# A graph network on one core: the two weightings of an attention step put together, and the second output's gate put behind the first one's

## The chip, the cores and the metric

The kernel runs on one core of a Trainium2 chip. The core has five engines with instruction queues of their own: TensorE (matrix products, "PE" in the profile; its weight loads are shown as "PEld"), VectorE ("DVE"), ScalarE ("ACT"), GpSimd ("POOL") and SyncE ("SP", which here issues DMAs). The metric is the time of one execution on the device in microseconds (us). The kernel before took 2346.37 us as the median of three runs (2345.69 to 2347.04).

## The reference

Per row, a layer normalisation and a rectification come first, then a batch normalisation, a graph convolution, four layers, a second graph convolution, and two residual sums. Cut to the two parts that the change touches, a layer is:

```
q = (xb @ Wq).reshape(BS, -1, H, DH)             # 16 graphs of 64 rows, 8 heads of 64
k = (cond @ Wk).reshape(BS, -1, H, DH)           # 16 x 256 rows of context
v = (cond @ Wv).reshape(BS, -1, H, DH)
w = softmax(einsum('bnhd,bmhd->bhnm', q, k) * DH ** -0.5)
o = einsum('bhnm,bmhd->bnhd', w, v)              # the weighting
h = h + (o @ Wo)
u = _ln(h) @ geglu_w[i] + geglu_b[i]             # 1024 x 512 times 512 x 4096
val, gate = jnp.split(u, 2, axis=-1)
f = val * gelu(gate)
h = h + f @ ffo_w[i] + ffo_b[i]
```

All data are 32-bit floats. The four layers run with weights of their own; the context `cond` is the same in all.

## The kernel before, in words

The four layers follow each other in one program. In each, the attention runs over eight steps, one for every 128 rows (two graphs) of the 1024. The projection of keys and values for step g + 1 is spread over step g, so that TensorE has work while the softmax of step g runs on VectorE and ScalarE.

Keys and values are exact to 32 bits, though the products are of 12-bit operands: each operand is split into a high and a low part and a third one (names `ah`, `al`, `as` for the left side, `bh`, `bl`, `bs` for the right), and a unit (`Twelve`) adds three groups of four products into one PSUM bank. `begin` issues the first two groups and asks ScalarE to scale the bank in place; `end` issues the third group, which must wait for that scaling, and copies the result out on ScalarE or VectorE. Units are staggered: the begin of the next stands between a unit's begin and its end.

`mix` weights the values. TensorE turns four blocks of the softmax (`tr_pr`); ScalarE and VectorE copy them to `pT`, turned block by turned block, ScalarE the even ones and VectorE the odd ones. Then `weigh(0)` and `weigh(1)` issue the small products of the first and the second half of the heads into one bank (`po`), 64 columns wide; the profile shows 32 products for each half. The last instruction copies the bank to `oT` on VectorE. Three hooks give `mix` other TensorE work to place in between. In steps 0 to 6 the first hook ends the last key unit, the second is empty, and the third begins the first value unit (`v[0]`) of step g + 1. In step 7 the second hook begins a product of the next stage, and the other two are empty.

The gated projection's first quarter is computed from plain 32-bit products (`Quad`), its other three quarters (r = 1 to 3, four chunks c each, 48 chunks in the four layers) by the class `Chunk`. A chunk makes a value and a gate block of two outputs with seven products instead of eight, by sums of operands. Six of the products (numbers 0, 5, 6, 4, 1, 3) are split into three groups as above: `scale` and `scale_onto` issue two groups and a scaling on ScalarE or VectorE, `end` the third group. The seventh is a plain 32-bit product (line 1175). `steps` is a generator; the loop over chunks runs the first five stretches of chunk n + 1 between the last three of chunk n. The gate of the second output (`g1`) needs product 4 and is made from VectorE's sum; the gate of the first output (`g0`) needs product 3. Both are one ScalarE instruction, at line 1139, of 128 x 512 elements. VectorE then multiplies each gate with its value block, at lines 1178 and 1181 (`fT`). Before it, ScalarE and VectorE split the operands of the chunks to come (`gha`, `gla`, `ghb`, `glb`), and GpSimd finishes that split and sums operands.

Order on TensorE in these parts is the order of the code, since nearly all of its instructions, and those of ScalarE and VectorE in the chunks, are marked to be kept in program order (`pin`). Waits between engines are put in by the framework, which leaves out a wait that an earlier wait of the same engine already covers. Instructions not marked so, such as the split of the first output operand (`left_parts`: `ah_f` on ScalarE, `al_f` and `as_f` on VectorE), are placed by the framework's scheduler.

Of the kernel before, what the change touches and what calls it, by code (L numbers as in the profile page):

```python
# [26 lines left out]
def gnn_kernel(  # L27
# [82 lines left out]
    def bank(name):  # L110
        return psum.tile([P, 512], F32, tag="bank", name=name)

    def t512(name, dtype=F32):
        return work.tile([P, 512], dtype, tag="t512", name=name)
# [83 lines left out]
    def transposed(t, name, each=lambda ins: ins):  # L198

        pt = bank(f"tr_{name}")  # L200
        for k in range(4):
            transposed.last = each(nc.tensor.transpose(pt[:, k * P:(k + 1) * P],
                                                       t[:, k * P:(k + 1) * P], ident))
        return pt
# [513 lines left out]
    with ExitStack() as behind:  # L718
        for begun_by in (scaled_last, shifted_last):
            behind.enter_context(tc.issue_after(begun_by.ins))  # L720
        for t in range(ET):
            if t % (ET // (NB * KC)) == 0:
                next(steps)
            count(t)
        for _ in steps:
            pass
        first_v = bank("begun_v0")
        plain(first_v, raw_x[0, 0], 0, raw_wv, range(2))
        with tc.issue_after(load_dve.ins):
            for j in counted:  # L730
                if j % 2:
                    degrees(j // 2, C[j // 2], t512(f"part_{j // 2}"))
        with tc.issue_after(degrees.last.ins):
            plain(first_v, raw_x[0, 0], 0, raw_wv, range(2, KC))
        nc.scalar.copy(begun["v0"][0][:, 0, :], first_v)
# [66 lines left out]
    def acc_tile(name):  # L802
        return accs.tile([P, 512], F32, tag="acc", name=name)
# [54 lines left out]
    def mix(l, g, probs, v, hooks, each=pin):  # L858

        oT = t512(f"oT_{l}_{g}")  # L860
        po = bank(f"po_{l}_{g}")

        def weigh(c2, pTs):
            for a in range(2):
                c = 2 * c2 + a
                for b in range(2):
                    for m in range(MB):
                        for j in range(2):
                            n0 = c * P + b * NPG
                            at = (a * MB + m) * P + b * NPG  # L870
                            each(nc.tensor.matmul(
                                po[j * DH:(j + 1) * DH, n0:n0 + NPG],
                                v[b][:, m, c * P + j * DH:c * P + (j + 1) * DH],
                                pTs[j][:, at:at + NPG],
                                start=(m == 0), stop=(m == MB - 1)))

        turned = []
        for c2 in range(2):
            pTs = []
            for j in range(2):  # L880
                u = 2 * c2 + j
                pt = transposed(probs[u], f"pr_{l}_{g}_{u}", each)
                pT = t512(f"pT_{l}_{g}_{u}")
                if j:
                    nc.vector.tensor_copy(pT, pt)
                else:
                    nc.scalar.copy(pT, pt)
                pTs.append(pT)
            turned.append(pTs)
            hooks[c2]()  # L890
        weigh(0, turned[0])
        hooks[2]()
        weigh(1, turned[1])
        mix.last = nc.vector.tensor_copy(oT, po)  # L894
        return oT

# [174 lines left out]
    class Chunk:  # L1071
# [69 lines left out]
        def steps(self, sum_next):  # L1141


            n, bias = self.n, gcols[:, self.cv:self.cv + 1]

            def add(to, x, y):
                pin(nc.vector.tensor_tensor(to, x, y, OP.add))  # L1147

            self.banks = {}
            self.scale(0)  # L1150
            yield
            self.scale(5)
            yield
            s1, u2, u3 = (acc_tile(f"g{x}_{n}") for x in ("s1", "u2", "u3"))
            pin(nc.scalar.copy(s1, self.end(0)))
            self.scale(6)
            yield
            add(u2, self.end(5), s1)
            yield
            sum_next()  # L1160
            self.scale(4)
            add(u3, self.end(6), u2)
            self.scale_onto(1, s1)
            g1 = acc_tile(f"g1_{n}")
            d = self.end(4)
            add(g1, d, u3)
            self.gate(g1, g1)
            self.scale_onto(3, u3)
            yield
            a = self.end(1)  # L1170
            yield
            g0 = acc_tile(f"g0_{n}")
            self.gate(g0, self.end(3))
            for k in range(2):
                pin(nc.tensor.matmul(d, self.last[:, k, :], self.rights[2][:, k, :], start=False,
                                     stop=k == 1, skip_group_check=True))
            f0, f1 = self.f.of(self.c)
            pin(nc.vector.scalar_tensor_tensor(f0, a, bias, g0, OP.add, OP.mult))
            add(d, d, u2)
            yield  # L1180
            pin(nc.vector.scalar_tensor_tensor(f1, d, bias, g1, OP.add, OP.mult))
            self.f.store(self.c)
# [263 lines left out]
    for l in range(L):  # L1446
# [118 lines left out]
        for g in range(NG - 1):  # L1565
# [19 lines left out]
            k[-2].end()  # L1585
            v = values(l, g + 1, wv)
            oTs.append(mix(l, g, probs, vs.pop(g), (k[-1].end, nothing, v[0].begin)))
            if g == NG - 2:
                ln3_norm(g - 2, g - 1, behind=mix.last)
# [49 lines left out]
        quads[0].first()  # L1639
        quads[1].first()  # L1640
        oT = mix(l, g, probs, vs.pop(g), (nothing, quads[2].first, nothing), lambda ins: ins)
        ln3_norm(g - 1)
        attn_out(l, g, oT, wo)
# [321 lines left out]
```

## Time and profile before

| What | Value |
|---|---|
| Median of three runs | 2346.37 us |
| Lowest and highest run | 2345.69 and 2347.04 us |
| The profiled execution | 2345.76 us |
| Its span, first to last instruction | 2343.9 us |
| TensorE busy | 2312.5 us, 12272 products |
| VectorE busy | 1624.6 us |
| ScalarE busy | 1081.7 us |
| GpSimd busy | 800.3 us |
| Granted TensorE clock | 1.00 |

The rows in the sections below have these columns. In a timeline: start in us from the span's start, duration in us, engine, line of the code and operation, what is written and read (buffer numbers left out), shape, count of merged instructions, and in brackets the engine's idle time ahead and what ended it. In a table of windows: the stretch of time, its length, then the busy time and number of instructions of TensorE, its weight loader, VectorE, ScalarE and GpSimd, the granted clock, and the share and rate of the DMA engines. In a row of waits: who waited for whom, us in total, how often, and the longest. Durations of matrix products include their modelled latency, so that neighbours overlap; times from start to start are the ones to add up.

### The profile page before, as it was taken

The page shows a single profiled execution, that of the slowest core. Times are in us where ns is not written, and L with a number is a line of the kernel's source. Part 1 is how long each engine was busy: PE and PEld are TensorE (multiplying, and loading weights), DVE is VectorE, ACT ScalarE, POOL GpSimd, SP SyncE. Part 2 cuts the span into 40 slices and gives each one's busy share as a digit, 9 for nine tenths or more (in the row PEclk, how much of TensorE's full clock was granted, in tenths as well). Part 3 has the DMA queues.
Part 4 walks back from the last instruction along what each step waited for, and adds up shares of the span by engine and source line. Part 5 has one row for each costly group of instructions (what it writes and reads, how often), then busy time and mean ns, then how long its engine had stood idle before and what let it go on. Part 6 is the DMA issues. An engine that isn't in the chain of part 4 may idle for free. (4 is left out here: it accounts for less than half of the span.)

```text
span 2343.9 us, 33537 instructions
## 1 busy us (share of the span) xinstructions
PE 2312.5 (99%) x12272; PEld 1716.5 (73%) x12272; DVE 1624.6 (69%) x3036; ACT 1081.7 (46%) x2099; POOL 800.3 (34%) x719
## 2 busy tenths in 40 slices
PE   8999999999999999999999999999999999999999
PEld 5668887577877887477886888567786888657787
DVE  9875456888974455788985544788886544688964
ACT  7444454455244445455344444555334444455410
POOL 1133222385032224177022333169022223158211
PEclk9999999999999999999999999999999999999999
DMA  6052120245412101144522101133531111033550
GB/s 202 12 165 73 67 74 8 70 126 174 151 62 68 42 19 37 54 119 137 180 73 68 66 21 37 34 106 117 180 126 68 43 44 37 7 115 116 180 190 37
DMA packets 161066, 205.40 MB, mean 88 GB/s; under 512 B 11304, under 2 KB 101744, under 8 KB 160896
## 3 DMA queue, kind: packets, MB, share of 16 engines
q1 hardware_dynamic: 158800, 197.77, 26.1%
q0 software_dynamic: 1376, 4.30, 0.5%
q8 instruction: 101, 1.65, 0.3%
q10 hardware_dynamic: 720, 1.11, 0.1%
q14 instruction: 69, 0.57, 0.1%
HBM read 152.80 MB, written 50.34 MB: 87 GB/s over the span
## 5 line engine op out<-in xcount | busy, mean ns | idle before, releaser
L321 POOL TENSOR_TENSOR as_c<-ah_c,al_c 128x512 fp32r<-128x512 f32 x128 | 196.9, 1568 | 409.3 <-PE fy L1258 234.4
L378 ACT ACTIVATE v<-v 128x512 f32<-128x512 f32 x127 | 74.1, 583 | 220.6 <-PE v L367 218.4
L1258 PE MATMUL fy<-bh_wff,ah_f 128*128 128x512 f32 x512 | 159.2, 392 | 0.0
L1258 PE MATMUL fx<-bs_wff,as_f 128*128 128x512 f32 x512 | 157.8, 389 | 0.5 <-DVE as_f L318 0.5
L1258 PE MATMUL fy<-bl_wff,al_f 128*128 128x512 f32 x512 | 157.8, 389 | 0.0
L315 ACT ACTIVATE ah_f<-fr 128x1024 fp32r<-128x1024 f32 x64 | 67.6, 1060 | 176.4 <-PE fy L1258 116.4
L1126 ACT ACTIVATE g<-g 128x512 f32<-128x512 f32 x192 | 111.9, 583 | 78.7 <-PE g L1112 78.7
L367 PE MATMUL v<-bh_wv,ah_c 128*128 128x512 f32 x508 | 145.9, 409 | 0.0
L367 PE MATMUL v<-bs_wv,as_c 128*128 128x512 f32 x508 | 143.4, 404 | 0.0
L848 ACT ACTIVATE pr<-sc,nmax 128x256 f32<-128x256 f32 x256 | 118.3, 475 | 53.6 <-DVE nmax L843 53.1
L1112 PE MATMUL g<-gr,gsa 128*128 128x512 f32 x384 | 137.1, 438 | 3.8 <-ACT g L1126 3.7
L378 ACT ACTIVATE k<-k 128x512 f32<-128x512 f32 x125 | 72.7, 585 | 144.5 <-PE k L367 144.5
L367 PE MATMUL v<-bl_wv,al_c 128*128 128x512 f32 x508 | 136.4, 390 | 0.0
L367 PE MATMUL k<-ah_c,bh_wk 128*128 128x512 f32 x500 | 134.6, 391 | 0.0
L367 PE MATMUL k<-al_c,bl_wk 128*128 128x512 f32 x500 | 134.0, 390 | 0.0
L367 PE MATMUL k<-as_c,bs_wk 128*128 128x512 f32 x500 | 132.1, 395 | 0.0
L1063 POOL TENSOR_TENSOR gsa<-gha,gla 128x512 fp32r<-128x512 f32 x88 | 112.1, 1295 | 55.6 <-DVE gla L1060 53.2
L1139 ACT ACTIVATE g<-g,gcols 128x512 f32<-128x512 f32 x96 | 67.2, 700 | 128.8 <-DVE g L1147 125.7
L1112 PE MATMUL g<-gr,gha 128*128 128x512 f32 x384 | 120.8, 396 | 0.0
L383 DVE COPY kT<-k 128x512 f32<-128x512 f32 x54 | 37.4, 692 | 118.9 <-PE k L367 118.9
L1112 PE MATMUL g<-gl,gla 128*128 128x512 f32 x384 | 118.6, 390 | 0.0
L920 POOL TENSOR_TENSOR os<-oT 128x256 f32<-128x256 f32 x12 | 8.8, 733 | 318.8 <-DVE oT L894 318.8
(353 smaller groups left out, 5749.4 us busy)
## 6 DMA issues: line engine op xcount, KB each, us to landing
f_dram<-fT SPq DMA_DIRECT2D x128, 256.0 KB, 2.7
fr<-f_dram SPq DMA_DIRECT2D x64, 512.0 KB, 4.4
ct<-cond_dram SPq DMA_DIRECT2D x48, 512.0 KB, 4.0
wff<-in_L_gnn_ffo_w_dram SPq DMA_DIRECT2D x32, 512.0 KB, 5.9
gxb<-in_L_gnn_geglu_w_dram SPq DMA_DIRECT2D x96, 128.0 KB, 2.6
gxa<-in_L_gnn_geglu_w_dram SPq DMA_DIRECT2D x96, 128.0 KB, 2.6
cond<-in_L_gnn_cond_dram SPq DMA_DIRECT2D x32, 256.0 KB, 3.4
cond_dram<-ct SPq DMA_DIRECT2D x16, 512.0 KB, 3.9
```

What stands on the lines that cost most here:

```text
L315: nc.scalar.mul(twelve_bits(h), x, INWARD * TINY)
L321: nc.gpsimd.tensor_tensor(twelve_bits(s)[:, k, :], h[:, k, :], l[:, k, :], OP.subtract)
L367: pin(nc.tensor.matmul(self.bank, twelve_bits(left[k // 2])[:, k % 2, self.c * P:(self.c + 1) * P], twelve_bits(right[k // 2])[:, k % 2, : ...
L378: nc.scalar.mul(self.bank, self.bank, 1.0 + TINY)
L383: nc.vector.tensor_copy(self.to(), self.bank)
L848: nc.scalar.activation(pr3[:, a, :], ps3[:, a, :], AF.Exp, bias=nmax[:, a:a + 1], accum_out=tot[:, a:a + 1])
L920: t.tensor_tensor(s1, a21, a22, OP.add)
L1063: pin(t.tensor_tensor(s_at, h_at, l_at, OP.subtract))
L1112: pin(nc.tensor.matmul(to, self.part(i, which)[:, k, :], self.rights[i][which].bitcast(F32R)[:, k, :], start=start and k == 0, stop=stop a ...
L1126: pin(nc.scalar.mul(to, to, 1.0 + TINY))
L1139: pin(nc.scalar.activation(to, of, AF.Gelu, bias=gcols[:, cg:cg + 1]))
L1258: pin(nc.tensor.matmul(to, twelve_bits(left[which][0])[:, k, b * P:(b + 1) * P], twelve_bits(right[which])[:, k, :], start=u == 0 and whic ...
```

## The change

Two edits:

```diff
@@ mix @@
             turned.append(pTs)
             hooks[c2]()
-        weigh(0, turned[0])
         hooks[2]()
-        weigh(1, turned[1])
+        for c2, pTs in enumerate(turned):
+            weigh(c2, pTs)
         mix.last = nc.vector.tensor_copy(oT, po)
@@ Chunk.steps @@
             g1 = acc_tile(f"g1_{n}")
             d = self.end(4)
             add(g1, d, u3)
-            self.gate(g1, g1)
             self.scale_onto(3, u3)
             yield
             a = self.end(1)
             yield
             g0 = acc_tile(f"g0_{n}")
             self.gate(g0, self.end(3))
+            self.gate(g1, g1)
```

The first edit puts the third hook, the begin of the next value unit, ahead of both weightings. On TensorE, in step 0 of layer 0, four groups of the value unit `v_1_0` appear behind the last turned block (the difference of the two orders, + is the changed kernel):

```order
 L202 MATMUL tr_pr_0_2_15737<-ident,pr_0_2_15653 128x128 x4
 L202 MATMUL tr_pr_0_3_15744<-ident,pr_0_3_15663 128x128 x4
+L367 MATMUL v_1_0_15751<-bh_wv_0_15057,ah_c_1_0_15501 128x512 x2
+L367 MATMUL v_1_0_15751<-bh_wv_1_15058,ah_c_1_1_15502 128x512 x2
+L367 MATMUL v_1_0_15751<-bl_wv_0_15059,al_c_1_0_15503 128x512 x2
+L367 MATMUL v_1_0_15751<-bl_wv_1_15060,al_c_1_1_15504 128x512 x2
 L871 MATMUL po_0_15717<-pT_0_0_15723,v_begun_456 64x64
 L871 MATMUL po_0_15717<-pT_0_1_15730,v_begun_456 64x64
```

They leave their old place between the two halves of the weighting, on the same engine, a few rows on:

```order
 L871 MATMUL po_0_15717<-pT_0_0_15723,v_begun_457 64x64
 L871 MATMUL po_0_15717<-pT_0_1_15730,v_begun_457 64x64
-L367 MATMUL v_1_0_15767<-bh_wv_0_15057,ah_c_1_0_15501 128x512 x2
-L367 MATMUL v_1_0_15767<-bh_wv_1_15058,ah_c_1_1_15502 128x512 x2
-L367 MATMUL v_1_0_15767<-bl_wv_0_15059,al_c_1_0_15503 128x512 x2
-L367 MATMUL v_1_0_15767<-bl_wv_1_15060,al_c_1_1_15504 128x512 x2
 L871 MATMUL po_0_15717<-pT_0_2_15742,v_begun_456 64x64
 L871 MATMUL po_0_15717<-pT_0_3_15749,v_begun_456 64x64
```

The two halves now stand in one run of products. The same move stands in each of steps 0 to 6 of each layer, 28 times; step 7 keeps its order.

The second edit moves one gate on ScalarE. Before, in layer 0, from the chunk (r, c) = (2, 0) to (2, 1), with the engines that each instruction waits for in brackets (a number in a name is layer-less: `g_0_2_0` is of chunk (2, 0); line 1126 is a scaling, 1139 a gate, 1155 the copy of product 0):

```order
L1139 ACTIVATE g_0_1_3_18760<-g_0_1_3_18704,gcols 128x512 [waits PE_49]
L1126 ACTIVATE g_0_2_0_18780<-g_0_2_0_18780 128x512 [waits PE_49]
L1139 ACTIVATE g_0_2_0_18795<-g_0_2_0_18795,gcols 128x512 [waits DVE_49,Activation_49]
L1126 ACTIVATE g_0_2_1_18806<-g_0_2_1_18806 128x512 [waits PE_49]
L1059 ACTIVATE ghb_2_1_18813<-gxb_2_1_18645 128x512 [waits DMAHW4_49,DMAHW3_49]
L1126 ACTIVATE g_0_2_1_18819<-g_0_2_1_18819 128x512 [waits PE_49]
L1059 ACTIVATE gha_2_2_18825<-gxa_2_2_18735 128x1024 [waits DMAHW3_49,Pool_49]
L1155 COPY gs_0_2_1_18840<-g_0_2_1_18806 128x512 [waits PE_49]
L1126 ACTIVATE g_0_2_1_18846<-g_0_2_1_18846 128x512 [waits PE_49]
L1139 ACTIVATE g_0_2_0_18852<-g_0_2_0_18800,gcols 128x512 [waits PE_49]
```

The same stretch of ScalarE in the changed kernel:

```order
L1139 ACTIVATE g_0_1_3_18699<-g_0_1_3_18699,gcols 128x512 [waits DVE_49]
L1126 ACTIVATE g_0_2_0_18780<-g_0_2_0_18780 128x512 [waits PE_49]
L1126 ACTIVATE g_0_2_1_18805<-g_0_2_1_18805 128x512 [waits PE_49,Activation_49]
L1059 ACTIVATE ghb_2_1_18812<-gxb_2_1_18644 128x512 [waits DMAHW4_49,DMAHW3_49]
L1126 ACTIVATE g_0_2_1_18818<-g_0_2_1_18818 128x512 [waits DVE_49,PE_49]
L1059 ACTIVATE gha_2_2_18824<-gxa_2_2_18734 128x1024 [waits DMAHW3_49,Pool_49]
L1155 COPY gs_0_2_1_18839<-g_0_2_1_18805 128x512 [waits DVE_49,PE_49]
L1126 ACTIVATE g_0_2_1_18845<-g_0_2_1_18845 128x512 [waits DVE_49,PE_49]
L1139 ACTIVATE g_0_2_0_18851<-g_0_2_0_18799,gcols 128x512 [waits DVE_49,PE_49]
L1139 ACTIVATE g_0_2_0_18795<-g_0_2_0_18795,gcols 128x512 [waits DVE_49]
```

The gate with the wait for VectorE alone has moved from ahead of the next chunk's first scaling to behind the first output's gate. The four instructions on the way have got a VectorE wait of their own, which the old gate's wait had covered.

One instruction of VectorE moves by the scheduler's choice, once in each layer: the split `al_f` of the first output operand, in the third chunk of the last quarter. Before:

```order
L1147 TENSOR_TENSOR gu_0_3_2_19305<-g_0_3_2_19309,gu_0_3_2_19304 128x512
L1130 TENSOR_SCALAR g_0_3_2_19339<-g_0_3_2_19339,gs_0_3_2_19303 128x512
L1147 TENSOR_TENSOR g_0_3_2_19345<-g_0_3_2_19330,gu_0_3_2_19305 128x512
L1130 TENSOR_SCALAR g_0_3_2_19350<-g_0_3_2_19350,gu_0_3_2_19305 128x512
L1235 TENSOR_SCALAR bl_wff_1_19133<-wff_1_18991,bh_wff_1_19132 128x512
L316 TENSOR_SCALAR al_f_0_0_19376<-ah_f_0_0_19375,fr_0_19273 128x1024
```

The same place on VectorE in the changed kernel:

```order
L1147 TENSOR_TENSOR gu_0_3_2_19304<-g_0_3_2_19308,gu_0_3_2_19303 128x512
L316 TENSOR_SCALAR al_f_0_0_19375<-ah_f_0_0_19374,fr_0_19272 128x1024
L1130 TENSOR_SCALAR g_0_3_2_19339<-g_0_3_2_19339,gs_0_3_2_19302 128x512
L1147 TENSOR_TENSOR g_0_3_2_19345<-g_0_3_2_19330,gu_0_3_2_19304 128x512
L1130 TENSOR_SCALAR g_0_3_2_19349<-g_0_3_2_19349,gu_0_3_2_19304 128x512
L1235 TENSOR_SCALAR bl_wff_1_19132<-wff_1_18990,bh_wff_1_19131 128x512
```

It now stands ahead of the two scalings at line 1130 instead of behind them. GpSimd's and SyncE's orders are unchanged, and no instruction is added to the computation or taken from it; some of the added waits are carried by wait instructions of their own.

## The prediction

> **What bounds the kernel now.** I read the page first, then the waits of TensorE and of its weight loader, then the stretches of time in which the two edited places lie.
>
> ```profile
> span 2343.9 us, 33537 instructions
> ...
> PE 2312.5 (99%) x12272; PEld 1716.5 (73%) x12272; DVE 1624.6 (69%) x3036; ACT 1081.7 (46%) x2099; POOL 800.3 (34%) x719
> ```
>
> TensorE is busy for 99% of the span and no other engine for more than 69%, so only what shortens or lengthens TensorE's own chain counts. Two rows show what of that chain is not arithmetic: a wait, and the idle time of the weight loader ahead of the 64-column products of the attention (tile po).
>
> ```profile
> PE g L1112 <- ACT g L1126: 3.7, 4, 1.1
> ```
> ```profile
> PEld po L871 <- issue: 17.7, 60, 0.8
> ```
>
> The numbers are microseconds in total, times, and the longest. The first row is four waits, one per layer, in the gated projection, on a ScalarE instruction of the line that does the scalings. The second row has 60 entries: two in each of the 28 attention steps that the diff reorders, one in each of the 4 last steps, which it leaves alone. "issue" means that nothing was waited for: it is the price of a border between two kinds of product. So both edits touch places where TensorE loses time now.
>
> **The change, part one: the weightings of an attention step.** This is TensorE's order in one step of layer 1; the other steps repeat it.
>
> ```profile
> 749.34 1.03 PE L202 MATMUL tr_pr<-ident,pr 128*128 128x128 f32 x8
> 750.12 1.18 PE L367 MATMUL k<-as_c,bs_wk 128*128 128x512 f32 x4
> 751.14 1.03 PE L202 MATMUL tr_pr<-ident,pr 128*128 128x128 f32 x8
> 752.10 1.15 PE L871 MATMUL po<-pT,v 128*64 128x64 f32 x32
> 753.18 1.20 PE L367 MATMUL v<-bh_wv,ah_c 128*128 128x512 f32 x4
> 754.22 1.08 PE L367 MATMUL v<-bl_wv,al_c 128*128 128x512 f32 x4
> 755.23 1.15 PE L871 MATMUL po<-pT,v 128*64 128x64 f32 x32
> 756.31 1.19 PE L367 MATMUL v<-bh_wv,ah_c 128*128 128x512 f32 x4
> ```
>
> Ends are modelled, so I count from start to start. From the last eight transposes to the first product of the next value unit it takes 756.31 - 751.14 = 5.17 us: transposes 0.96, weighting 1.08, value unit 2.05, weighting 1.08. The edit puts the value unit ahead of the first weighting. The three pieces of the new order are all in the trace: eight transposes followed by a 512-column product take 750.12 - 749.34 = 0.78; the value unit, followed by a weighting, takes 755.23 - 753.18 = 2.05; and 64 weightings in one run stand in the last step of each layer:
>
> ```profile
> 2023.89 2.08 PE L871 MATMUL po<-pT,v 128*64 128x64 f32 x64
> 2025.90 1.12 PE L298 MATMUL ga<-ln3T,wval 128*128 128x512 f32 x2
> ```
>
> That is 2.01, against 2 x 1.08 in two runs. The sum is 0.78 + 2.05 + 2.01 = 4.84, a gain of 0.33 per step and of 28 x 0.33 = 9.2 us. Nothing is computed less; two of the four changes into and out of the narrow products are gone.
>
> The rule that speaks against it is in the Trainium skill, "TensorE: Matmul & The Clock Gate", Part 2, "Step-by-step: what each phase is for": the engine's queue pulls weight loads ahead of running matmuls, so that the next weights load behind the present product. By that alone a border would cost nothing and this part would be worth 0. The 17.7 us of the weight loader's row say otherwise, and "TensorEngine Tiling (Array Packing)", "Key Properties", says why: "Mode switching requires drain". By this rule the 9.2 us stand, and the trace sides with it.
>
> What could take the gain away is the data. The second half of the weighting needs the fourth turned block, which VectorE copies last:
>
> ```profile
> 753.15 0.69 DVE L885 COPY pT<-tr_pr 128x512 f32<-128x512 f32 x1
> ```
>
> It is there at 753.84. In the new order the second half starts at 751.14 + 0.78 + 2.05 + half of 2.01 = 754.97, so 1.13 us remain (1.39 today). The first half needs blocks copied earlier still. The value unit's own ScalarE scaling, due before that unit's third group, gets its input sooner than now. The orders of VectorE, ScalarE, POOL and SP in the attention do not move. One more wait, for a VectorE copy long done, goes ahead of the first weighting. The trace has no such wait at this border. Its bounds are 0 and 0.17 us a step, the latter the width of a whole border here (0.96 against 0.78 behind the transposes); I take 0, because TensorE drains there anyway. So the part is worth 4.5 to 9.8 us (the upper end if the value unit also starts 0.02 quicker, the 1.02 of the products at 750.12 against the 1.04 at 753.18).
>
> **Part two: the gate of the second output.** In the projection ScalarE now stands at the gate (line 1139) until VectorE has made its input, and the scaling of the next chunk's first product is queued behind it. Where VectorE is late, TensorE gets to the product's last group and finds it unscaled. First ScalarE, then TensorE, in the second chunk of layer 0:
>
> ```profile
> 470.36 0.72 ACT L1139 ACTIVATE g<-g,gcols 128x512 f32<-128x512 f32 x1 [3.92 <-DVE g L1147]
> 470.99 0.58 ACT L1126 ACTIVATE g<-g 128x512 f32<-128x512 f32 x1
> 471.50 0.61 ACT L1059 ACTIVATE ghb<-gxb 128x512 fp32r<-128x512 f32 x1
> ```
> ```profile
> 468.85 0.61 PE L1112 MATMUL g<-gl,gla 128*128 128x512 f32 x2
> ...
> 470.21 0.61 PE L1112 MATMUL g<-gr,gsb 128*128 128x512 f32 x2
> 471.71 0.70 PE L1112 MATMUL g<-gr,gsa 128*128 128x512 f32 x2 [0.88 <-ACT g L1126]
> ```
>
> The product to be scaled is done at 469.46; its scaling starts at 470.99, because the gate sat ahead of it. With the gate moved, the scaling can run at about 469.5 to 470.1, and the group at 471.71, due 0.45 after 470.21 (the spacing of the three groups from 468.85 on), meets no wait. The size is read from whole periods of a chunk (from one last product to the next), not from the wait alone, since the pipeline must refill too:
>
> ```profile
> 462.56:473.61 11.05, 10.17 (x41) 7.44 (x40) 8.18 (x11) 6.46 (x11) 9.03 (x11) 1.00 0.35 96
> 473.61:483.54 9.93, 9.93 (x42) 7.51 (x40) 8.52 (x11) 5.42 (x10) 7.91 (x9) 1.00 0.53 160
> ...
> 493.49:503.69 10.20, 10.17 (x42) 7.43 (x41) 9.51 (x12) 6.25 (x11) 8.25 (x9) 1.00 0.35 103
> ...
> 1004.32:1015.38 11.06, 10.19 (x41) 7.44 (x40) 8.18 (x11) 6.48 (x11) 9.03 (x11) 1.00 0.36 98
> 1546.09:1557.40 11.31, 10.17 (x41) 7.44 (x40) 7.88 (x11) 6.45 (x11) 9.28 (x11) 1.00 0.35 98
> 2087.84:2098.88 11.04, 10.18 (x41) 7.43 (x40) 8.21 (x11) 6.47 (x11) 9.01 (x11) 1.00 0.33 96
> ```
> ```profile
> 2118.75:2128.95 10.20, 10.19 (x42) 7.43 (x41) 9.52 (x12) 6.25 (x11) 8.25 (x9) 1.00 0.34 103
> ```
>
> An undisturbed period is 9.93. The first period of the four layers is longer by 1.12 + 1.13 + 1.38 + 1.11 = 4.74, and the fourth (first and last of four shown) by 0.27 in these two and by 0.82 in all four, by the same late gate. The sum is 5.5 us. The ends are 3.7 (the waits alone) and 6.0 (a few hundredths more in other chunks).
>
> What does the gate meet at its new place? It follows the first output's gate, and the scaling of the next sum stands behind it. The tightest case is a chunk in which ScalarE also splits an output weight; ScalarE, then VectorE's multiplication that needs the moved gate:
>
> ```profile
> 495.23 0.67 ACT L1139 ACTIVATE g<-g,gcols 128x512 f32<-128x512 f32 x1
> 496.78 0.58 ACT L1126 ACTIVATE g<-g 128x512 f32<-128x512 f32 x1 [0.88 <-PE g L1112]
> ```
> ```profile
> 497.80 0.74 DVE L1181 SCALAR_TENSOR_TENSOR fT<-g,gcols,g 128x512 f32<-128x512 f32 x1
> ```
>
> ScalarE idles 0.88 there for TensorE, and the gate takes 0.67 to 0.72: it ends near 496.6, 0.2 before the scaling can start and 1.2 before VectorE asks. Cost 0. In a layer's last chunk the moved gate delays the split of a later output operand by as much, behind which VectorE still has its own multiplications to do: 0 too.
>
> Two side effects. ScalarE's instructions that leaned on the old gate's wait now carry a VectorE wait of their own, about four per chunk, all for work of the chunk before. The nearest row is the split at 471.50, which waits for two DMAs: it starts 0.51 behind the start of a 0.58 us scaling, so at once. I price them at 0; the trace bounds it by ScalarE's idle time. And once per layer VectorE now does a 1.22 us split of the first output operand (al_f) ahead of, not behind, the scaling that an ending product (561.07) needs:
>
> ```profile
> 558.08 0.70 DVE L1130 SCALAR_TENSOR_TENSOR g<-g,gs 128x512 f32<-128x512 f32 x1
> ...
> 560.66 1.22 DVE L316 SCALAR_TENSOR_TENSOR al_f<-ah_f,fr 128x1024 fp32r<-128x1024 f32 x1
> ```
> ```profile
> 561.07 0.61 PE L1112 MATMUL g<-gr,gsb 128*128 128x512 f32 x2
> ```
>
> The scaling would end at 558.78 + 1.22 = 560.0 against 561.07: covered by 1.07. If that cover were gone, the four splits would cost at most 4.9 us.
>
> **The sum.** 9.2 + 5.5 = 14.7. The profiled execution took 2345.76 us (its span and 1.86 around it), so 2331.1; the median of the runs, 2346.37, stands 0.6 above it: 2331.7 us.
>
> **The rivals.** The gate's wait goes but VectorE's lateness shows at the next thing: TensorE then waits for a VectorE scaling instead. For it: VectorE is busy for 9.5 of 10.2 us in the slow fourth period. Against it: in the second chunk no wait for VectorE stands beside the ScalarE one. Then 2346.4 - 9.2 = 2337.2. Chance 8%.
>
> The added waits cost at the borders: attention 4.5, projection 4: 2337.9. Chance 6%. That such waits become instructions of their own is said by the Trainium skill, "Perfetto Trace Analysis", "Identifying Dependency Chains", without a price.
>
> Borders cost nothing in themselves, or the narrow products pay the same in one run: the attention keeps its time, 2340.9. Against it stands the 2.01. Chance 5%.
>
> Slower: the fourth turned block is late. VectorE copies it behind a 1.2 us split of the context; if the new timing held it up, each step would wait. The gain of a step is eaten at 1.13 + 0.33 = 1.46 us of delay, and at 1.13 + 0.33 + (5.5 + 4.7) / 28 = 1.82 us the kernel is 0.2% slower, 2351 or more. Nothing in the trace delays it so. Chance 4%.
>
> Neither edit moves TensorE's chain: 2346. Chance 4%.
>
> **How the numbers follow.** My case has 73%, its own range 2329.5 to 2334.5. Within 0.2% (4.7 us, about what a measurement tells from nothing) is 4%, slower 4%, and all the rest, 92%, is faster. The range 2329.5 to 2338.5 takes in my case and the two rivals near 2337 and leaves out the others.
>
> **What would show it.** The 32-product runs of po become runs of 64, the weight loader's idle row falls from 60 entries to 32 and to some 13 us; the row of TensorE's wait on the scaling disappears; the first chunk period falls from 11.05 to 9.93; TensorE's share stays at 99%. I am wrong if a wait of TensorE on VectorE's copies of the turned blocks appears, if the period between attention steps stays, or if the first chunk period keeps its length under another name.

## The result: 2330.35 us, 0.7% faster, and the profile after

The changed kernel takes 2330.35 us (median of 6 runs, 2329.82 to 2330.77) against 2346.27 us before (6 runs, 2345.65 to 2347.04). The ratio is 0.9931, 95% interval 0.9921 to 0.9942. The forecast was 2331.7, with a range of 2329.5 to 2338.5. The profiled execution took 2330.63 us, its span 2328.8. In the fences of this part are the rows of the changed kernel that answer to those shown of the kernel before. First its page:

```profile
span 2328.8 us, 33792 instructions
...
PE 2300.4 (99%) x12272; PEld 1714.9 (74%) x12272; DVE 1613.3 (69%) x3036; ACT 1078.3 (46%) x2099; POOL 817.7 (35%) x719
```

TensorE is still busy for 99% and still sets the time. It does the same 12272 products in 12.1 us less busy time; the 255 instructions more are waits that became instructions. Next the weight loader's idle time ahead of the narrow products (total, times, longest), and the waits of TensorE:

```profile
PEld po L871 <- issue: 13.2, 32, 0.8
```
```profile
PE gc L298 <- DVE gu L1013: 7.3, 4, 1.8
...
PE g L1112 <- DVE g L1130: 1.3, 4, 0.3
```

The loader's entries went from 60 to 32 and its 17.7 us to 13.2. In TensorE's list the row "g L1112 <- ACT g L1126" is gone (it held 3.7 us), no other row has taken its place, and no wait for a turned block is there. This is TensorE's order in one attention step, and then the stretches of the first and fourth chunk of layer 0 and the first of layer 1 (start and end, length, busy time of TensorE, weight loader, VectorE, ScalarE and GpSimd, granted clock, DMA share, GB/s):

```profile
747.62 1.03 PE L202 MATMUL tr_pr<-ident,pr 128*128 128x128 f32 x8
748.42 1.17 PE L367 MATMUL v<-bh_wv,ah_c 128*128 128x512 f32 x4
749.43 1.08 PE L367 MATMUL v<-bl_wv,al_c 128*128 128x512 f32 x4
750.44 2.08 PE L871 MATMUL po<-pT,v 128*64 128x64 f32 x64
752.45 1.20 PE L367 MATMUL v<-bh_wv,ah_c 128*128 128x512 f32 x4
```
```profile
460.97:470.90 9.93, 9.93 (x42) 7.51 (x40) 7.89 (x11) 6.64 (x11) 8.53 (x10) 1.00 0.28 83
...
490.75:500.68 9.93, 9.93 (x42) 7.51 (x40) 8.82 (x11) 6.28 (x11) 9.29 (x8) 1.00 0.35 105
...
998.73:1008.66 9.93, 9.93 (x42) 7.51 (x40) 7.89 (x11) 6.64 (x11) 8.53 (x10) 1.00 0.28 85
```

From the last eight transposes to the next value unit it takes 752.45 - 747.62 = 4.83 us; it was 5.17, and 4.84 was forecast. Every full chunk period is 9.93, where it was up to 11.31. Counted over the trace, the steps of the attention gave 9.7 us (from the transposes of a layer's first step to those of its eighth 2.43 less, four times) and the projection 6.0 (from the first chunk's last product to the twelfth's, a layer took 108.13 and takes 106.62). These are 15.7 of the 15.9 by which the medians differ; the spans differ by 15.0, since the profiled execution after had spent 0.85 more ahead of the first chunk (0.4 in a wait for VectorE at the start of the kernel, 0.5 in one ahead of tile gd in layer 0). In another profiled execution of the same kernel, below, that stretch was 0.8 shorter.

### The profile page after: what moved, and what is told of

Read it like the earlier page. It is cut to its first block, busy times and chain, and to the rows that moved or that the text cites. A ratio compares the mean times of both kernels' runs of the same rounds, so it can differ in the third digit from the quotient of the medians.

```text
span 2328.8 us, 33792 instructions
## 1 busy us (share of the span) xinstructions
PE 2300.4 (99%) x12272; PEld 1714.9 (74%) x12272; DVE 1613.3 (69%) x3036; ACT 1078.3 (46%) x2099; POOL 817.7 (35%) x719
## 5 line engine op out<-in xcount | busy, mean ns | idle before, releaser
L1126 ACT ACTIVATE g<-g 128x512 f32<-128x512 f32 x192 | 112.9, 588 | 191.9 <-PE g L1112 191.9
L1112 PE MATMUL g<-gr,gsa 128*128 128x512 f32 x384 | 136.2, 436 | 0.0
L1112 PE MATMUL g<-gr,gha 128*128 128x512 f32 x384 | 120.7, 395 | 0.0
L1112 PE MATMUL g<-gl,gla 128*128 128x512 f32 x384 | 118.6, 390 | 0.0
L1258 PEld LDWEIGHTS fy<-bh_wff,ah_f 128*128 128x128 f32 x512 | 96.1, 188 | 21.6 <-issue 1.9
```

The source lines that it names most:

```text
L1112: pin(nc.tensor.matmul(to, self.part(i, which)[:, k, :], self.rights[i][which].bitcast(F32R)[:, k, :], start=start and k == 0, stop=stop a ...
L1126: pin(nc.scalar.mul(to, to, 1.0 + TINY))
L1258: pin(nc.tensor.matmul(to, twelve_bits(left[which][0])[:, k, b * P:(b + 1) * P], twelve_bits(right[which])[:, k, :], start=u == 0 and whic ...
```

## The experiments

**Each edit alone.** The first run has only the edit of the attention, the second only that of the projection.

```diff
 # e1_mix: the kernel before, with
-        weigh(0, turned[0])
         hooks[2]()
-        weigh(1, turned[1])
+        for c2, pTs in enumerate(turned):
+            weigh(c2, pTs)
 # e2_gate: the kernel before, with
-            self.gate(g1, g1)
             self.scale_onto(3, u3)
...
             self.gate(g0, self.end(3))
+            self.gate(g1, g1)
```

> The kernel before with the first edit alone: the value unit ahead of both weightings, the gate left where it was. Theory (a removed pair of borders is worth 0.35 us in each of 28 steps, and has nothing to do with the projection): 9.9 us faster than before, 2346.3 - 9.9 = 2336.4, with the four waits of TensorE on the scaling (3.7 us) and first chunk periods of 11.0 to 11.3 still there. Rival (part of the 9.9 is only to be had together with the moved gate, for instance because the projection begins in another phase): less than 8 us, above 2338.

> The kernel before with the second edit alone: the gate moved, the two weightings on either side of the value unit as before. Theory (the gate held the scalings behind it, and every chunk that ran long ran long for that): 6.0 us faster, 2340.3, all chunk periods 9.93, no wait of TensorE on a scaling. Rival (only the waits that the profile lists are won, the rest came with the attention): 3.7 us, 2342.6.

Measured: 2336.75 us (ratio 0.9962, 0.9949 to 0.9976) and 2340.52 us (0.9976, 0.9967 to 0.9985) against 2346.43 before, so 9.7 and 5.9 us. Together that is 15.6, and both edits at once gave 15.9: they add up, and neither needs the other. In the first run's list of waits the row of the scaling stands, and its first chunk is as long as before:

```profile
PE g L1112 <- ACT g L1126: 3.4, 4, 0.9
```
```profile
460.74:471.79 11.05, 10.19 (x41) 7.44 (x40) 8.19 (x11) 6.47 (x11) 9.03 (x11) 1.00 0.33 96
```

In the second run it is gone with the attention as it was, so the projection's whole gain comes from the gate's place:

```profile
464.66:474.59 9.93, 9.93 (x42) 7.51 (x40) 7.89 (x11) 6.64 (x11) 8.53 (x10) 1.00 0.26 79
```

**More borders.** If a border has a price, putting more of them in has to cost it again. Here the 64 narrow products of a step are cut into four runs of 16.

```diff
 # e3_quarters: the changed kernel, with
         def weigh(c2, pTs):
             for a in range(2):
+                if len(hooks) > 3:
+                    hooks[3](2 * c2 + a)
...
-(k[-1].end, nothing, v[0].begin)
+(k[-1].end, nothing, nothing, v[0].quarter)
```

`quarter` issues two of the eight products of the value unit's begin, ahead of each run; its own code is not shown.

> The changed kernel with more borders: the 64 narrow products of each of the 28 steps in four runs of 16, with two of the value unit's eight products ahead of each run. The same products, the same data, later needed than made. Theory (a pair of borders has a price of its own, 0.35 us): three pairs more in each step, 28 x 3 x 0.35 = 29 us slower than the changed kernel, 2359.8, and slower than the kernel before; the weight loader's idle row of the narrow products is back with some 200 entries. Rival (the gain came from the place of the value unit or from what VectorE and ScalarE get done meanwhile, the borders being free): 2330.4 within 3 us.

Measured: 2359.93 us, ratio 1.0055 (1.0038 to 1.0072), 29.6 us more than the changed kernel. Over 28 x 3 = 84 pairs that is 0.35 a pair. TensorE's order, one step:

```profile
727.14 0.71 PE L386 MATMUL v<-bh_wv,ah_c 128*128 128x512 f32 x2
727.78 0.69 PE L888 MATMUL po<-pT,v 128*64 128x64 f32 x16
728.39 0.73 PE L386 MATMUL v<-bh_wv,ah_c 128*128 128x512 f32 x2
...
732.22 1.20 PE L367 MATMUL v<-bh_wv,ah_c 128*128 128x512 f32 x4
```
```profile
PEld po L888 <- issue: 33.6, 88, 0.8
...
PEld po L888 <- ACT pT L904: 10.2, 28, 0.4
```

TensorE's own list has no wait at any of these starts, and the step's piece takes 732.22 - 727.14 = 5.08 where the changed kernel takes 752.45 - 748.42 = 4.03. So the price belongs to the border itself, not to the place of the value unit. The loader's entries stand in two rows, 116 in all and not 200: four for each of the 28 steps and one for each of the 4 last. The second row names ScalarE's copy of a turned block for the first run of each step, but in this step that copy ended at 727.57, 0.2 ahead of the run's first load at 727.77, and the loader was idle for 0.36 there as at the three other runs. So this is no wait for data either. Together the rows hold 43.8 us, 30.6 more than in the changed kernel: here, with 512-column products on both sides of every run, the loader's idle time follows the price of 29.6 us.

**Only narrow products?** Transposes and 512-column products also differ in kind, but both use all 128 columns. Here sixteen transposes stand in one run.

```diff
 # e6_turns: the changed kernel, with
-(k[-1].end, nothing, v[0].begin)
+(nothing, k[-1].end, v[0].begin)
```

> The changed kernel with one more regrouping of the same kind: the four products that end the last key unit come behind the second eight transposes, not between the two groups of eight, so that a step has sixteen transposes in one run. Theory (each change of kind costs TensorE time, the narrow products being only the dearest): the four products between transposes take 1.01 us in a step against 0.91 between their like, so at least 0.10 a step is won, 28 x 0.10 = 2.8 us, 2327.6, and with a second border of the size of that one 5.6, 2324.8. Rival 1 (only the 64-column products pay at their borders): 2330.4, no change. Rival 2 (the second transposes now wait for their banks or the turned blocks come late): a wait of TensorE or longer steps, slower than 2331.

Measured: 2329.80 us, ratio 0.9929 (0.9915 to 0.9943), 0.5 below the changed kernel, within what these runs can tell apart. The trace gives 0.03 us a step:

```profile
717.10 1.91 PE L202 MATMUL tr_pr<-ident,pr 128*128 128x128 f32 x16
718.76 1.17 PE L367 MATMUL k<-as_c,bs_wk 128*128 128x512 f32 x4
...
721.68 2.08 PE L871 MATMUL po<-pT,v 128*64 128x64 f32 x64
```

The piece takes 721.68 - 717.10 = 4.58; in the changed kernel the same products take 4.61 (0.79 + 1.01 + 0.79 + 2.02). My 0.10 was misread: the 1.01 behind the transposes holds the tail of the eighth transpose, since eight of them take 0.79 ahead of another product and sixteen take 718.76 - 717.10 = 1.66, not 1.58. The first rival holds: of the borders tried, only those into and out of the 64-column products have a price. The Trainium skill, "TensorEngine Tiling (Array Packing)", "Key Properties", has it so: a change of the tiling mode drains TensorE. The trace agrees, with 0.35 for a pair of borders between the whole array (128*128 in the rows: transposes and 512-column products) and half its columns (128*64: the weightings), and 0.03 for a pair that stays on the whole array.

The weightings differ from their neighbours in two more ways, and the profile of the changed kernel has rows for both. They are plain 32-bit products between split ones. So are the four of line 1175 in a chunk, on the whole array:

```profile
500.68 1.88 PE L1175 MATMUL g<-ln3T,gy 128*128 128x512 f32 x4
501.99 1.02 PE L1112 MATMUL g<-gr,gsa 128*128 128x512 f32 x2
502.85 0.63 PE L1112 MATMUL g<-gr,gha 128*128 128x512 f32 x2
```

These six take 502.85 - 500.68 = 2.17. Four plain products among their like take 1.72 (427.18 to 428.90 in the same profile) and two split ones 0.46 (502.85 to 503.31), so nothing is left for this pair of borders. The weightings are also short. At 36.89, seven 16-bit products on the whole array, of 384, 352, 32, 288, 96, 224 and 160 columns, take 0.66 us up to the next product, and their starts lie 0.16, 0.15, 0.03, 0.12, 0.04 and 0.10 apart: the one of 32 columns between two long ones brings no pause, so a change of length alone has no such price there. What is left is the 64 columns of the array. No run changed these alone.

**How late may the fourth turned block be?** VectorE's copy is made twice, then four times.

```diff
 # e4_late1 (2) and e5_late3 (4): the changed kernel, with
                 if j:
-                    nc.vector.tensor_copy(pT, pt)
+                    for _ in range(2 if c2 and g < 7 else 1):
+                        nc.vector.tensor_copy(pT, pt)
```

> The changed kernel with VectorE's copies of the second output of each pair's later block made twice, so that the fourth turned block of each of the 28 steps is 0.65 us later. In the changed kernel it is there 0.1 to 0.2 us ahead of the first narrow product, the half that needs it starts 1.0 behind that: a margin of 1.1 to 1.2 us (0.65 in the first step of layer 0). Theory: the delay is covered, 2330.4 within 0.7 us. Rival (the margin is not where the start times put it, for instance since the narrow products of both halves are queued with one wait at the head): 28 x 0.5 = 14 us slower, about 2344.

> The same with that copy made four times: the fourth turned block is 1.95 us later in each of the 28 steps. Theory: 1.95 - 1.15 = 0.8 us are not covered, 28 x 0.8 = 22 us slower than the changed kernel, 2353, with a wait of TensorE on VectorE's copy in the trace. Rival 1 (the slack is wider): under 10 us slower. Rival 2 (no slack at all): 28 x 1.8 = 50 us slower, 2381.

Measured: 2330.41 us for the first (ratio 0.9929, 0.9913 to 0.9946): one copy more, 0.72 us, is covered as predicted. VectorE, then TensorE:

```profile
749.11 1.41 DVE L886 COPY pT<-tr_pr 128x512 f32<-128x512 f32 x2
```
```profile
749.91 2.08 PE L871 MATMUL po<-pT,v 128*64 128x64 f32 x64
751.93 1.20 PE L367 MATMUL v<-bh_wv,ah_c 128*128 128x512 f32 x4
```

The block is there at 750.52, 0.6 behind the start of the narrow products, and they take 2.02 all the same. Only the first step of layer 0, whose copy is later, lost 0.19.

The second took 2376.94 us (1.0129, 1.0112 to 1.0146), 46.6 more than the changed kernel and twice my 22. The wait has the name I gave it:

```profile
PE po L871 <- DVE pT L886: 32.4, 24, 2.4
```

The size has three parts. A copy takes 0.72 from start to start, not 0.65, so three take 2.16, and 1.1 was not covered in 12 of the steps. In 12 others VectorE's order itself changed in my kernel: one half of the context's split now stands between the copies, so the block was 1.2 later still and the step lost 2.2 (2.7 in layer 0's first). The 4 last steps lost 0.24. These make 26.6 + 13.4 + 1.0 = 41 us, as does the sum over all runs of narrow products in the trace. VectorE and TensorE in layer 1:

```profile
731.62 1.41 DVE L886 COPY pT<-tr_pr 128x512 f32<-128x512 f32 x2
732.95 1.26 DVE L316 SCALAR_TENSOR_TENSOR al_c<-ah_c,ct 128x1024 fp32r<-128x1024 f32 x1
734.13 1.40 DVE L886 COPY pT<-tr_pr 128x512 f32<-128x512 f32 x2
```
```profile
735.59 1.15 PE L871 MATMUL po<-pT,v 128*64 128x64 f32 x30 [1.90 <-DVE pT L886]
736.66 1.87 PE L367 MATMUL v<-bh_wv,ah_c 128*128 128x512 f32 x4
738.34 1.91 PE L367 MATMUL v<-bl_wv,al_c 128*128 128x512 f32 x4
```

The third part, some 4.7 us, is in the last two rows and is told at the end: TensorE's clock fell.

**The gate half way.** Which of the work behind the gate mattered?

```diff
 # e7_gate_mid: the changed kernel, with
             yield
+            self.gate(g1, g1)
             a = self.end(1)
...
             self.gate(g0, self.end(3))
-            self.gate(g1, g1)
```

> The changed kernel with the gate of the second output half way: in ScalarE's order behind the two scalings and the two splits that it stood ahead of before, but still ahead of the copy, the next scaling and the first output's gate. Theory (only the scalings queued right behind the gate mattered): as fast as the changed kernel, 2330.4, within 0.7 us; all chunk periods 9.93. Rival (the gate has to be out of the way of all that ScalarE does before the first output's gate, since VectorE is late by more than two scalings): it waits again in the first chunk of each layer, between 1 and 4.5 us slower, 2331.4 to 2334.9.

Measured: 2331.28 us (0.9941, 0.9927 to 0.9954), 0.9 above the changed kernel and a little outside the 0.7 that I allowed; its profiled execution has a span of 2328.4, no longer than 2328.8. First chunk, then ScalarE ahead of it:

```profile
460.18:470.18 10.00, 10.00 (x42) 7.52 (x41) 8.37 (x11) 6.64 (x11) 8.60 (x10) 1.00 0.25 75
```
```profile
460.36 1.06 ACT L1059 ACTIVATE gha<-gxa 128x1024 fp32r<-128x1024 f32 x1 [1.56 <-POOL gxa L1096]
461.33 0.71 ACT L1139 ACTIVATE g<-g,gcols 128x512 f32<-128x512 f32 x1
```

The gate starts right behind the split, without a wait of its own, and the first period of a layer is 10.00: four layers lose about 0.4 us, of 6.0. So the theory holds for nearly all of it: what the old gate cost was the two scalings and the two splits that stood right behind it. The other half microsecond of the median is not to be seen in the trace.

**A further version.** The score products (tile sc, 64 x 64) are narrow too. Two kernels put those of the next step right behind the weightings: in all steps, then only in three steps of a layer, with the sixteen transposes as above. The changed kernel ran again beside the second.

```diff
 # e8_joined: the changed kernel, with
-            probs = scores(l, g, qT, kTs.pop(g))
+            probs = scored or scores(l, g, qT, kTs.pop(g))
...
             oTs.append(mix(l, g, probs, vs.pop(g), (k[-1].end, nothing, v[0].begin)))
+            scored = scores(l, g + 1, qT, kTs.pop(g + 1))
 # e9_joined_even: the same for g in (0, 2, 4), and
-(k[-1].end, nothing, v[0].begin)
+(nothing, k[-1].end, v[0].begin)
```

> The changed kernel with the 32 score products of the next step (tile sc, 64 rows by 64 columns) put right behind the 64 weighting products, instead of behind the value units, so that the narrow products of a step stand in one stretch. Theory (a border between 128-column and 64-column products has a price, 0.35 a pair for po, some 0.25 for sc, 1.00 + 1.05 against 2 x 0.91 for the products around them): one pair of the two goes and a smaller border between the two narrow kinds stays, 0.1 to 0.3 us a step won, 3 to 8 us, 2322 to 2328, if ScalarE's eight exponentials, which now stand ahead of the scalings of the value units, are done in time. Rival (they are not, and TensorE waits for the scaling of a value unit or for a bank): slower than 2332.

> The changed kernel with two regroupings: the next step's score products right behind the weightings in the three steps of a layer (0, 2, 4) that have no output products behind them, and the sixteen transposes in one run. The first was worth 0.18 us a step where nothing waited (27.96 to 27.78 from one step's transposes to the next), 12 x 0.18 = 2.2; the second 0.02 x 28 = 0.6. Theory (the 7 us lost when all steps were joined came from the steps with output products, whose scores no longer covered VectorE's sums): 2330.4 - 2.8 = 2327.6, no wait of TensorE on those sums. Rival (something else in the joined order costs, such as the exponentials ahead of the scalings): 2330 or more.

> The changed kernel once more, on the same chip as the run beside it: 2330.4 within 0.7 us.

Measured: 2337.35 us for the first (0.9961, 0.9947 to 0.9974), 7.0 slower than the changed kernel. Its order, and what went wrong in the steps with output products:

```profile
722.13 2.08 PE L871 MATMUL po<-pT,v 128*64 128x64 f32 x64
724.14 1.96 PE L836 MATMUL sc<-kT,qT 64*64 64x256 f32 x32
726.03 1.19 PE L367 MATMUL v<-bh_wv,ah_c 128*128 128x512 f32 x4
```
```profile
766.47 1.03 PE L298 MATMUL ocd<-wo_sums,oT 128*128 128x256 f32 x4
768.10 1.10 PE L298 MATMUL ocd<-wo,om 128*128 128x256 f32 x4 [0.61 <-DVE hall L952]
```

The score products used to stand between these two groups and covered VectorE's sum; without them TensorE waits. In layer 1 the three steps with output products are 0.64 to 0.66 us longer each, the one behind them 0.31, and the three others 0.12 to 0.18 shorter: 1.95 + 0.31 - 0.42 = 1.8 us. Layers 2 and 3 lose 1.9 each and layer 0 only 0.1, since the wait on the sum stands in one of its steps (10 times in all, 6.1 us). That is 5.8 of the 7.0 us; the rest is not in the steps. The rival's sign was right, and its cause in part. Most of the loss comes from the sum, but the weight loader now also waits for ScalarE's scaling of a value unit, 20 times and 5.6 us in all, with 0.62 in the last of each layer's joined steps; the changed kernel has no such row. A joined step without output products gains 0.1 to 0.2, the low end of my 0.1 to 0.3.

The second took 2330.05 us (2328.20 to 2330.40; 0.9927, 0.9914 to 0.9941), the changed kernel beside it 2330.33 (2329.85 to 2331.97; 0.9931, 0.9917 to 0.9945). The wait on the sum is gone, but the gain is 0.3 of the 2.8 expected and the runs overlap: the rival's 2330 or more. In the profiled execution, the quickest of the five, the steps gained 1.8 us. The rival's cause is in the trace as well: the weight loader waits 16 times, 3.5 us in all, for a value unit's scaling that stands behind the exponentials. In layer 1 the joined steps take 27.77, 27.85 and 28.11 us against 27.96. In the third the exponentials began 0.3 later than in the same step of layer 2, which takes 27.85, and the loader's wait for the scaling was 0.48 instead of 0.21; why they began later is open. It is no version that can be said to beat the changed kernel.

## Why the prediction was right, step by step

- **The border between the narrow and the wide products has a price of its own.** Shown, by taking pairs away (9.7 us for 28) and by putting 84 in (29.6 us). The forecast of 0.33 a step was 0.34 to 0.35. The sum of the attention, 9.2, came out at 9.7, near the upper bound of 9.8: I had the pieces right, but the value unit was quicker by the 0.02 that I named for that end.
- **Bounds of the added wait.** I took 0 of 0 to 0.17 us a step (0.96 - 0.78 is 0.18), and the step's 4.83 leaves no room for more than 0.
- **The margin of the fourth turned block.** Forecast 1.13. In the changed kernel the copy ends 0.12 to 0.19 ahead of the narrow products in most steps and the half that needs it starts 1.0 behind them, so 1.1 to 1.2; in layer 0's first step it ends 0.35 behind, which I had not looked for. The delays of 0.72 and 2.16 put the point between them. The rival of the late block was a real mechanism that this order does not reach.
- **The gate.** The term was sized 5.5 and measured 5.9 to 6.0: I took the first and fourth periods and gave away the hundredths in the others, which were of the same cause. That is a mis-sized term; with the attention's it makes up 1.0 of the 1.2 us that the gain of 15.9 lies above my 14.7. The product's last group now starts without a wait:

```profile
469.08 0.61 PE L1112 MATMUL g<-gr,gsa 128*128 128x512 f32 x2
```

- **The place that the gate went to.** ScalarE does both gates together and is idle behind them; the next scaling waits for TensorE, not for the gate:

```profile
471.43 1.29 ACT L1139 ACTIVATE g<-g,gcols 128x512 f32<-128x512 f32 x2
474.19 0.58 ACT L1126 ACTIVATE g<-g 128x512 f32<-128x512 f32 x1 [1.47 <-PE g L1112]
```

- **VectorE's split moved ahead of two scalings.** TensorE's wait on them stayed at 1.3 us in 4 times, so the cover of 1.07 held.
- **The rivals.** No wait on VectorE took the gate's place (2337.2), the added waits cost nothing that can be seen (2337.9), the borders are not free (2340.9), both edits reach TensorE's chain (2346). Of the signs that I named one was loosely chosen: the loader's row fell to 13.2 as said, but by 4.5 us of the 9.7. In the kernel before, the run behind the transposes showed only 0.17 of idle time in that row (at 752.10) and the one behind the value unit 0.36 (at 755.23), so I should not have read its 17.7 us as the price of the borders.

## What to carry to other kernels

On a kernel whose TensorE never rests, look at the order of kinds of product: here each round trip into 64-column products cost 0.35 us, the price of some 11 of those products, whatever data was ready, while a pair of changes between transposes and 512-column products cost 0.03 at most. Price it by whole stretches from start to start, with all pieces moved, since the first product behind a border carries the tail of the kind before it. On an engine that keeps the order of the code, find what stands behind an instruction that waits for a late input: moving that one instruction past its followers gave back more than the wait that the profile listed (6.0 against 3.7), as long as its own reader is later still.

## What the runs showed of the hardware that I had not expected

In the kernel with four copies TensorE waited 1.90 us in the first step of layer 1. Behind that wait products ran at about half their speed: eight took 740.04 - 736.66 = 3.38 us, where the eight behind another wait of nearly the same length took 805.52 - 803.58 = 1.94. The first two rows are the 3.41 us that hold this wait and the 3.41 us behind them; the last two are the same for a wait of 1.84 us in layer 0 (busy time of TensorE behind the comma, granted clock third from the end):

```profile
733.51:736.92 3.41, 1.51 (x37) 1.30 (x33) 2.14 (x4) 0.00 (x0) 3.41 (x3) 1.00 0.68 232
736.92:740.33 3.41, 3.41 (x9) 2.64 (x9) 0.54 (x1) 0.00 (x0) 0.87 (x1) 0.50 0.08 31
245.40:248.81 3.41, 1.57 (x47) 1.36 (x41) 2.23 (x3) 0.00 (x0) 3.41 (x3) 1.00 0.02 5
248.81:252.22 3.41, 3.41 (x16) 2.83 (x16) 0.69 (x1) 0.95 (x2) 1.13 (x1) 1.00 0.01 2
```

The granted clock was 0.50 for 3.41 us and 1.00 again from 740.34 on. The first steps of layers 1, 2 and 3 had this, about 1.6 us lost in each; a wait of 2.37 us in layer 0 and the others of some 1.84 did not. The slow stretches begin at 736.92, 1286.47 and 1836.02, so 549.55 us apart, which is 161 times 3.413. The Trainium skill, "TensorE: Matmul & The Clock Gate", Part 1, speaks of a free-running window of about 3.4 us over which activity is judged, with half the clock after a window of idleness. The length and the spacing of the slow stretches agree with such a window. That a wait of 1.90 us was enough does not agree with a whole window of idleness.

Counted on that grid, the trace also tells the three steps from the others. Ahead of each slow stretch TensorE was busy for 1.50 or 1.51 of the window's 3.41 us. The two windows that held a whole wait of 1.84 us had 1.57, and the wait of 2.37 us was cut by the grid at 177.13, so that the later window had 1.65; none of these was followed by a slower clock. So in this kernel the limit lies between 1.51 and 1.57 us of busy time in a window. That fits all 24 waits, and the profile of the run with the gate alone, which has 1.32 busy from 82.36 to 85.77 and a clock of 0.50 up to 89.19; no run was made to test it.
